# Layer 1, third wavelet level: five shifts on two quarters of the array, two partial sums added by the product above

## The chip, the cores and the metric

The kernel runs on one core of a Trainium2 chip. The metric is the device time of one execution in microseconds (us). Three runs of the kernel before took 5713.84, 5716.87 and 5730.83 us; the median is 5716.87. One more execution was taken with the profiler; it took 5714.57 us, and its profile spans 5712.6 us of that.

## The reference, cut to what matters

The program is four convolutional layers in sequence on 32 images of 96 channels, 56 by 56, each with a group norm in front and a residual sum behind. Layers 0, 2 and 3 are not touched. Layer 1 is a depthwise 5x5 convolution plus a three-level Haar wavelet transform, with a depthwise 5x5 convolution on the four bands of each level:

```
for i in range(3):
    co = haar2d(cur)                      # ll, lh, hl, hh at half the size
    cur = co[:, :, 0]                     # ll goes to the next level
    level_coeffs.append(dwconv(co, wconv_w[i]) * wscale[i])
next_ll = 0
for i in reversed(range(3)):
    co = level_coeffs[i]; co[:, :, 0] += next_ll
    next_ll = ihaar2d(co)                 # back up to twice the size
y = x + dwconv(x, base_w) * base_scale + base_b + next_ll
```

At the third level an input to the level is 14 rows by 14 columns for each image and channel.

## The kernel before

**How layer 1 is tiled.** Channels are taken in 48 pairs. In a pair, rows and column phases of an image lie on SBUF partitions and the 32 images on the free axis. A depthwise convolution down the rows is then a product with a banded (Toeplitz) matrix, one for each shift along the columns; TensorE adds the shifts in PSUM. All matrices are f32, and the profile shows every f32 product as two weight loads and two matmuls, which the text calls two passes. A product with f32r operands is one.

**The steps of a pair.** `lowest1` (L894) makes the input of level 2 out of `xh` and `xl`, two parts of the normalized image: `high` (ScalarE, L877) rounds `x` to `xh`, and `low` (VectorE, L881) makes `xl`, the rest. `lowest2` (L903) makes `x3`, the input of level 3, with the matrix `low2`: 112 rows by 56 columns, for both channels of the pair. `level3` (L910) forms five shifts with `T3`, a 56x56 block-diagonal matrix for each shift (channel 0 in rows and columns 0 to 27, channel 1 in 28 to 55), and ScalarE copies the sum to `c3` (L913). `level2` (L920), for each channel, forms three shifts and then adds the third level by one more product, `up2` times `c3` (L921), with 56 rows by 128 columns. The eviction of its sum is by halves: ScalarE copies a half, rounded (L926), then VectorE takes the rest (L927). `level1` (L938 for the product up, L932 for the three shifts) ends in `y`, which VectorE forms (L951) and SyncE's queue stores.

**What sets the order.** TensorE, VectorE, ScalarE and SyncE keep the order of the program here (`manual_schedule`). The loop at the end of `layer1` works on three pairs at a time: `far` is normalized, `nxt` goes through levels 2 and 3, and `i` through level 1. On TensorE one turn is: `lowest1(nxt)`, `level1(i, 0, 0)`, `lowest2(nxt)`, `level1(i, 0, 1)`, `level3(nxt)`, `level1(i, 1, 0)`, `level2(nxt, 0)`, `level2(nxt, 1)`, `level1(i, 1, 1)`. The first step of the next turn, `lowest1`, needs the `xl` that `low(far, 1)` makes, which on VectorE stands behind the four L927 of `level2`. On ScalarE `level3`'s copy is followed by the copies of `matrices1(far, 1)` (seven instructions, L748 and L775), then `high(far, 1)`, then the L926 of `level2`.

**Loads.** SyncE's queue issues all transfers of the layer. `load(i + 3)` brings, for each channel, the images, factors, matrices and, in `third` (L841), 28 rows of `T3`. Three sets of `T3`, `T2` and `c2` are filled with zeros by GpSimd when the layer begins (L820).

**Tiles on the array.** Layer 2's depthwise convolution already runs on four quarters of the array, 64 rows by 64 columns each. Its `quarter` picks row half `r` and column half `c`; in `depthwise` it is called as `quarter(ps[x], k, t, r, r ^ x, j, ...)`, so that for `x = 0` the quarters (0, 0) and (1, 1) write partitions 0 to 63 and 64 to 127 of the same PSUM tile, in the same half `j`, which is one bank. In layer 0 `project` runs eight tiles of 64 rows by 32 columns in f32 (the rows `hc,wg` of L548).

Of the kernel before, what the change touches and what calls it, by code (L numbers as in the profile page):

```python
# [10 lines left out]
F32 = mybir.dt.float32  # L11
BF16 = mybir.dt.bfloat16
F32R = mybir.dt.float32r
# [7 lines left out]
B, C, H, W = 32, 96, 56, 56  # L21
# [9 lines left out]
HH = H // 2  # L31
PH = HH * NPH
# [596 lines left out]
NK = 3  # L629
LEN = 2 * (HH + HALO) - 1  # L630
MIDL = HH + HALO - 1
KW = 5
# [100 lines left out]
def load_halves(nc, X, y):  # L733


    nc.sync.dma_start(X[:PH].rearrange("p h b q -> p h (b q)"), y.rearrange("(h p) b q -> p h (b q)", h=2))
    rows = y.rearrange("(t p r) b q -> t p r (b q)", t=NP, p=NPH)
    for h, v in enumerate((rows[2, :, :HALO], rows[1, :, -HALO:])):
        nc.sync.dma_start(X[PH:, h].rearrange("p b q -> p (b q)"), v)
# [11 lines left out]
def shifts(n, ks):  # L751


    for d in sorted(range(-(ks // 2), ks // 2 + 1), key=abs):
        yield ks // 2 + d, slice(max(0, -d), n - max(0, d)), slice(max(0, d), n + min(0, d))
# [5 lines left out]
def load_matrices(nc, pool, t, c, raw=None):  # L761

    if raw is None:
        raw = pool.tile([128, 2, NK * PH], F32, tag="raw", name="raw")
    nc.sync.dma_start(raw[:, 0], t[c, :128])
    nc.sync.dma_start(raw[LOW:PH, 1], t[c, LOW:PH])
    nc.sync.dma_start(raw[PH:, 1], t[c, 128:])
    return raw
# [11 lines left out]
def load_norm(nc, pool, norm, c):  # L780
    nr = pool.tile([128, 2 * B + 1], F32, tag="nr", name="nr")
    nc.sync.dma_start(nr, norm[c : c + 1, :].to_broadcast([128, 2 * B + 1]))
    return nr
# [3 lines left out]
def layer1(ctx, tc, w, y0, left, made, norm, t1, t2, t3, y1, k2, behind):  # L787
# [4 lines left out]
    nc = tc.nc  # L792
# [3 lines left out]
    pool = ctx.enter_context(tc.tile_pool(name="l1", bufs=2, reuse_waits="tile"))  # L796
    pfine = ctx.enter_context(tc.tile_pool(name="l1pf", bufs=4, space=PSUM, reuse_waits="tile"))
    psum = ctx.enter_context(tc.tile_pool(name="l1p", bufs=4, space=PSUM, reuse_waits="tile"))
    N2, N3 = W4 // 2, W4 // 2

    def constant(name, shape):
        t = cp.tile(shape, F32, tag=name, name=name)
        nc.sync.dma_start(t, w[name])
        return t

    def rounded(name, shape):

        t = cp.tile(shape, F32R, tag=f"{name}r", name=f"{name}r")
        nc.scalar.copy(t, constant(name, shape))
        return t  # L810
# [3 lines left out]
    for i in reversed(range(NF)):  # L814
        sets[i] = {
            name: cp.tile(shape, dtype, tag=f"{name}{i}", name=f"{name}{i}") for name, shape, dtype in (
                ("T3", [2 * HH, 2, HH * KW], F32), ("T2", [PH, 2, NK, 128], F32), ("c2", [128, 2, 2, N2, B], F32R))}
    for d in sets:
        for t in d.values():
            nc.gpsimd.memset(t.bitcast(F32) if t.dtype == F32R else t, 0.0)  # L820
# [1 line left out]
    def load(i):  # L822

        st = {"i": i, **sets[i % NF], "X": [], "T": [None] * 2, "nr": [], "raw": [], "raw2": [], "pf": {}}

        def images(c):
            X = io.tile([128, 2, B, W4], F32, tag="X", name="X", bufs=8)
            load_halves(nc, X, y0[c // GR][c % GR])
            st["X"].append(X)

        def factors(c):
            st["nr"].append(load_norm(nc, norms, norm, c))

        def matrices(c):
            st["raw"].append(load_matrices(nc, pool, t1, c))
            raw = pool.tile([PH, NK * PH], F32, tag="raw2", name="raw2", bufs=4)
            nc.sync.dma_start(raw, t2[c])
            st["raw2"].append(raw)

        def third(c):  # L840
            nc.sync.dma_start(st["T3"][c % 2 * HH : (c % 2 + 1) * HH, c % 2], t3[c])  # L841

        if i == 0:
            for c in range(2):
                matrices(c)
            left.issue(NP)
            for c in range(2):
                images(c)
            made.store(norm)
            for c in range(2):  # L850
                third(c)
            return st
        for c in (2 * i, 2 * i + 1):
            images(c)
            factors(c)
            matrices(c)
            third(c)
        left.issue(1)
        return st
# [38 lines left out]

    def lowest2(st):

        ps = psum.tile([2 * HH, N3, B], F32, tag="w", name="pa2")
        for j in range(2):
            nc.tensor.matmul(ps, low2[:, j, :], st["x2"][:, j], start=(j == 0), stop=(j == 1))  # L903
        st["x3"] = pool.tile([2 * HH, N3, B], F32, tag="x3", name="x3", bufs=2)
        nc.scalar.copy(st["x3"], ps)

    def level3(st):
        ps = psum.tile([2 * HH, N3, B], F32, tag="w", name="pc3")
        for n, (k, to, of) in enumerate(shifts(N3, KW)):
            nc.tensor.matmul(ps[:, to], st["T3"].rearrange("x c y -> x (c y)")[:, k::KW], st["x3"][:, of],  # L910
                             start=(n == 0), stop=(n == KW - 1))
        st["c3"] = pool.tile([2 * HH, N3, B], F32, tag="c3", name="c3", bufs=2)
        nc.scalar.copy(st["c3"], ps)  # L913

    def level2(st, j):

# [46 lines left out]
    def begin(st):  # L963
        for j in range(2):
            matrices1(st, j)
        for j in range(2):
            matrices2(st, j)
        both = cp.tile([128, 2, 2 * B + 1], F32, tag="nr0", name="nr0")
        made.spread(both, pick, psum.tile([128, 2, 2 * B + 1], F32, tag="w", name="pr0"))
        st["nr"] = [both[:, j, :] for j in range(2)]  # L970
        for j in range(2):
            for h in range(2):
                normal(st, j, h)
                st["pf"][j, h] = pfine.tile([128, W4, B], F32, tag="f", name="pc1")
                fine(st, j, h, True)
            high(st, j)
        for j in range(2):
            low(st, j)
# [3 lines left out]
    def do(step, i, *args):  # L982
        if i in sts:
            step(sts[i], *args)

    with tc.manual_schedule(engines=MANUAL_SP):
        low1 = rounded("low1", [128, 2, 2, 128])
        up1 = rounded("up1", [128, 2, 2, 128])
        low2 = constant("low2", [PH, 2, 2 * HH])
        up2 = constant("up2", [2 * HH, 2, 128])  # L990
        pick = constant("pick", [C, 2, 128])
        for i in range(-3, PAIRS):
            nxt, far = i + 1, i + 2
            if i + 3 < PAIRS:
                sts[i + 3] = load(i + 3)
            if far == 0:
                begin(sts[0])
                continue
            do(lowest1, nxt)
            do(normal, far, 0, 0)  # L1000
            do(matrices1, far, 0)
            do(normal, far, 0, 1)
            do(level1, i, 0, 0)
            do(lowest2, nxt)
            do(high, far, 0)
            do(low, far, 0)
            do(matrices2, far, 0)
            do(normal, far, 1, 0)
            do(level1, i, 0, 1)
            do(level3, nxt)  # L1010
            do(matrices1, far, 1)
            do(normal, far, 1, 1)
            do(high, far, 1)
            do(level1, i, 1, 0)
            do(level2, nxt, 0)
            do(level2, nxt, 1)
            do(matrices2, far, 1)
            do(low, far, 1)
            do(level1, i, 1, 1)
            sts.pop(i, None)  # L1020
            behind(i)
# [548 lines left out]
def lowest_bands():  # L1570

    low1 = np.zeros((PH + HALO * NPH, 2, 2, 128), np.float32)
    low2 = np.zeros((PH, 2, 2 * HH), np.float32)
    up1 = np.zeros((128, 2, 2, 128), np.float32)
    up2 = np.zeros((2 * HH, 2, 128), np.float32)

    def at(r, p):
        return PH // 2 * (r // 14) + 14 * p + r % 14  # L1580

    for r in range(HH):
        for p in range(NPH):
            for h in range(2):
                for n in range(2):
                    low1[at(r, p), h, n, at(HH // 2 * h + r // 2, 2 * n + p // 2)] = 0.5
            for c in range(2):
                low2[at(r, p), c, HH * c + 2 * (r // 2) + p // 2] = 0.5
    n = PH // 2
    for i in range(2):  # L1590
        for h in range(2):
            up1[64 * i : 64 * i + n, h, :, :PH] = low1[:PH, h, :, n * h : n * h + n].transpose(2, 1, 0)
        up2[:, :, 64 * i : 64 * i + n] = low2[n * i : n * i + n].transpose(2, 1, 0)
    return {"low1": low1, "low2": low2, "up1": up1, "up2": up2}


def layouts(a):
# [34 lines left out]
    def phase_taps(v):  # L1632
# [49 lines left out]
        "group": group.astype(np.float32),  # L1682
        "pick": np.repeat(np.eye(C, 2, dtype=np.float32)[:, :, None], 128, axis=2),
        **lowest_bands(),
        "grid": np.broadcast_to(grid, (C,) + grid.shape),
    }
# [23 lines left out]
```

## Time and profile before

| what | value |
|---|---|
| median of three runs | 5716.87 us |
| profiled execution | 5714.57 us, span 5712.6 us |
| layer 1 in the span | about 2640 to 3570 us |
| one turn of layer 1 (L894 to L894, 2997.66 to 3015.68) | 18.02 us |
| busy: TensorE, VectorE, ScalarE | 96%, 82%, 73% of the span |
| L903: 4 passes for each pair, 192 in all | 112x56 weights, 112x224 moving |
| L910: 10 passes for each pair, 480 in all | 56x56 weights; 224, 192 and 160 moving columns |
| L921: 4 passes for each pair, 192 in all | 56x128 weights, 56x224 moving |
| ScalarE copies from PSUM | 339 ns for 224 elements a partition (L905, L913), 532 ns for 448 (L897) |

A row of the costliest groups reads: line, engine, operation, output and inputs, the rows and columns of the weights (56*56), the shape and count; then the busy time in us, the mean of one in ns, and the idle time before it with what ended it. In a timeline a row is a start in us, a duration in us, and a group of instructions that follow each other; PE is a matmul, PEld a weight load. A matmul's end is modelled, so that the distance of starts says more than durations.

### The profile page before, as it was taken

Reading aid. Unit: us, or ns where it says so; the run is one execution under the profiler, and the core shown is the slowest. Engines: PE = TensorE matmul, PEld = TensorE weight load, DVE = VectorE, ACT = ScalarE, POOL = GpSimd, SP = SyncE. Lnnn points to the kernel's source line nnn. Section 1 sums busy time; section 2 is a strip of 40 time slices with the busy share of each in tenths; the row PEclk is TensorE's granted clock in tenths of the full one; section 3 lists DMA queues with packets and bytes.
Section 4 is the critical chain, followed back from the end, with each engine's and each line's share of the span. In section 5 each row is a group of like instructions: output and inputs, shape, how many; then the busy total and the mean of one; then the engine's idle time right before and its main releaser. Section 6 shows DMA issues by size and latency. Waiting matters only on the chain.

```text
span 5712.6 us, 137352 instructions
## 1 busy us (share of the span) xinstructions
PE 5494.4 (96%) x59704; PEld 3068.1 (54%) x59704; DVE 4692.3 (82%) x5413; ACT 4174.0 (73%) x6024; POOL 240.6 (4%) x158
## 2 busy tenths in 40 slices
PE   5999999999999999997999999899999999998999
PEld 2333333343343333333566665777788777776444
DVE  6999999999999999997776665777777777775777
ACT  5888888888888888884556654777777777676455
POOL 5000000000000000000000000000000000000000
PEclk9999999999999999998999999999999999999999
DMA  3123333332222332214577666479588796763888
GB/s 99 16 56 61 60 59 58 57 58 44 53 53 59 62 56 55 51 22 60 145 152 150 149 147 123 21 53 51 40 55 46 49 53 40 51 47 38 236 249 247
DMA packets 1285740, 454.45 MB, mean 80 GB/s; under 512 B 1102977, under 2 KB 1281081, under 8 KB 1283217
## 3 DMA queue, kind: packets, MB, share of 16 engines
q1 hardware_dynamic: 1285137, 445.68, 50.1%
q8 instruction: 468, 7.67, 0.6%
q14 instruction: 135, 1.11, 0.1%
HBM read 283.77 MB, written 214.08 MB: 87 GB/s over the span
## 4 chain that ended last, share of the span: by engine, by line
PE 81%; DMA 6%; ACT 4%; DVE 4%; issue 2%; SPq 1%; POOL 1%; ACTq 0%; DVEq 0%; POOLq 0%
PE psd L493 17%; PE psd L1291 13%; PE psj L548 10%; PE ps L426 7%; PE pc L932 7%; PE ps L1272 6%; PE pse L449 6%; PE psj L1334 3%; DMA X<-y 3%; PE pc L920 2%; ACT hi L1242 2%; PE pa L894 2%; PE pc L1466 2%; PE pc L910 1%; DMA raw<-tdiff 1%
## 5 line engine op out<-in xcount | busy, mean ns | idle before, releaser
L467 DVE SCALAR_TENSOR_TENSOR h<-hpad,l_wdw,h 128x3136 f32<-128x3136 f32 x512 | 1782.2, 3481 | 9.1
L493 PE MATMUL psd<-plane,filt 128*32 128x392 f32 (+5 forms) x16384 | 1083.6, 485 | 0.0
L1291 PE MATMUL psd<-apad,diag 64*64 64x392 bf16 x20736 | 916.2, 330 | 67.7 <-issue 63.8
L1291 PEld LDWEIGHTS <-diag 64*64 64x64 bf16 x20736 | 687.5, 106 | 291.7 <-issue 117.0
L493 PEld LDWEIGHTS psd<-plane,filt 128*32 128x32 f32 (+1 forms) x16384 | 390.7, 108 | 674.0 <-issue 621.6
L1262 ACT ACTIVATE u<-ps,o,s 128x784 int16<-128x784 f32 x576 | 536.4, 1002 | 163.9 <-PE ps L1272 145.0
L1262 ACT ACTIVATE a<-psd,o,s 128x784 int16<-128x784 f32 x448 | 423.6, 998 | 279.4 <-PE psd L1291 279.4
L748 ACT COPY T<-raw 128x112 f32<-128x112 f32 (+2 forms) x1386 | 445.6, 385 | 221.9 <-DMA raw<-tdiff 164.1
L426 PE MATMUL ps<-xn,l_wboth 96*128 96x392 f32 (+1 forms) x1536 | 465.2, 505 | 23.8 <-ACT xn L408 22.9
L467 DVE SCALAR_TENSOR_TENSOR hc<-hhalf,l_wdw,hc 128x1568 f32<-128x1568 f32 x256 | 473.7, 1850 | 16.1 <-ACT hc L460 9.5
L1272 PE MATMUL ps<-hi,l_w1q 96*128 96x392 f32 x1280 | 463.2, 362 | 6.8 <-DVE u L1260 3.7
L932 PE MATMUL pc<-x,T 128*112 128x416 f32 (+1 forms) x1152 | 447.3, 525 | 5.9 <-DVE x L870 5.9
L1272 PE MATMUL ps<-lo,l_w1q 96*128 96x392 f32 x1280 | 438.3, 342 | 2.9 <-DVE lo L1250 2.9
L1466 PE MATMUL pc<-x,T 128*112 128x416 f32 (+1 forms) x1152 | 419.4, 525 | 15.0 <-DVE x L1459 10.5
L449 PE MATMUL pse<-xn,l_wboth 96*32 96x392 f32 x4096 | 391.9, 501 | 3.6 <-ACT hab L470 3.6
L426 PEld LDWEIGHTS ps<-xn,l_wboth 96*128 96x128 f32 (+1 forms) x1536 | 219.5, 173 | 248.2 <-issue 53.6
L1466 PEld LDWEIGHTS pc<-x,T 128*112 128x112 f32 x1152 | 203.5, 178 | 230.4 <-issue 185.0
L470 ACT ACTIVATE hab<-psd,o,s 128x784 f32<-128x784 f32 x256 | 283.7, 1113 | 58.5 <-PE psd L493 56.1
L436 ACT ACTIVATE hpad<-ps,o,s 128x784 f32<-128x784 f32 x256 | 278.4, 1104 | 49.2 <-PE ps L426 47.8
L548 PE MATMUL psj<-h,wg 128*32 128x392 f32 x3072 | 307.1, 514 | 0.2 <-DVE wg L535 0.2
L548 PE MATMUL psj<-hab,wg 128*32 128x392 f32 x3072 | 304.8, 509 | 0.0
L453 ACT ACTIVATE plane<-pse,o,s 128x784 f32<-128x784 f32 x256 | 255.9, 1000 | 25.0 <-PE pse L449 20.3
(266 smaller groups left out, 7643.5 us busy)
## 6 DMA issues: line engine op xcount, KB each, us to landing
X<-y SPq DMA_DIRECT2D x192, 392.0 KB
y<-xt SPq DMA_DIRECT2D x108, 392.0 KB
y<-y SPq DMA_DIRECT2D x96, 392.0 KB
out_dram<-y SPq DMA_DIRECT2D x96, 392.0 KB
twav<-zwav SPq DMA_DIRECT2D x768, 36.8 KB
y<-kept SPq DMA_DIRECT2D x72, 392.0 KB
xt<-y SPq DMA_DIRECT2D x59, 392.0 KB
xt<-in_x_dram SPq DMA_DIRECT2D x8, 2352.0 KB
```

The costliest lines, as they stand in the source:

```text
L426: nc.tensor.matmul(ps[p, j, :NT], wexp[:, k * 128 : k * 128 + 128][:, m], im["xn"][:, j, rows, :].rearrange("c h w -> c (h w)"), start=Tru ...
L449: nc.tensor.matmul(ps[f * GC : (f + 1) * GC, half, :NT].rearrange("p (r w) -> p r w", w=W2), wexp[:, c : c + GC], im["xn"][:, f % 2, r0 : ...
L467: nc.vector.scalar_tensor_tensor(h2, taken(im, k, t), wdw[:, k, t : t + 1], h2, ALU.mult, ALU.add)
L470: nc.scalar.activation(view, ps, AF.Silu, bias=bi[1][:, c : c + 1], scale=sc[1][:, c : c + 1], accum_out=accum)
L493: nc.tensor.matmul(ps[at * GC : (at + 1) * GC, r, :NT].rearrange("p (r w) -> p r w", w=W2)[:, r0 - half * n : r1 - half * n, q0:q1], filt[ ...
L548: nc.tensor.matmul(ps[s * GC : (s + 1) * GC, t, :NT].rearrange("c (m r q) -> c r q m", m=2, q=W4), wg[p, k, c * GC : (c + 1) * GC], phases ...
L748: nc.scalar.copy(to.rearrange("x t (p s) -> x t p s", p=NPH), v[:, k])
L932: nc.tensor.matmul(ps[:PH, to], st["T"][j][:, h, k, :], st["x"][:, j, h, of], start=first and n == 0, stop=not first and n == NK - 1)
L1262: nc.scalar.activation(out, ps, AF.Identity, bias=o[:, c : c + 1], scale=s[:, c : c + 1])
L1272: nc.tensor.matmul(ps[:, j, :NT], w1[:, k * 128 : k * 128 + 128], im[part][:, r0 : r0 + RT, :].rearrange("c h w -> c (h w)"), start=(part ...
L1291: nc.tensor.matmul(ps[q, j, :NT].rearrange("p (r w) -> p r w", w=W), diag[p, k, t, :], v, start=(t == 0), stop=(t == 8))
L1466: nc.tensor.matmul(ps[:, :, to], st["T"][:, h, k, :], st["x"][:, h, :, of], start=(n == 0), stop=(n == NK - 1))
```

## The change

`low2` and `up2` get twice the columns and rows: each is padded from 56 to 64 and repeated, so `lowest2` writes `x3` twice, on partitions 0 to 63 and 64 to 127, and `up2` adds the two halves of `c3`. `T3` holds the block-diagonal matrix twice in the same way. The shifts `k` = 2, 3, 4 run on the quarter of rows and columns 0 to 63, `k` = 0, 1 on that of 64 to 127, into the two halves of one PSUM tile. The upper half's first column is not written by either of its two shifts, so the copy to `c3` leaves it out and `c3` becomes a tile of the set, filled with zeros once. `third` issues two transfers for each channel where it issued one.

```diff
-                ("T3", [2 * HH, 2, HH * KW], F32), ("T2", ...), ("c2", ...))}
+                ("T3", [128, 64 * KW], F32), ("T2", ...), ("c2", ...),
+                ("c3", [128, N3, B], F32))}
...
         def third(c):
-            nc.sync.dma_start(st["T3"][c % 2 * HH : (c % 2 + 1) * HH, c % 2], t3[c])
+            at, n = c % 2 * HH, HH * KW
+            for tile in range(2):
+                nc.sync.dma_start(st["T3"][64 * tile + at : 64 * tile + at + HH, at * KW : at * KW + n], t3[c])
...
     def lowest2(st):
-        ps = psum.tile([2 * HH, N3, B], F32, tag="w", name="pa2")
+        ps = psum.tile([128, N3, B], F32, tag="w", name="pa2")
...
     def level3(st):
-        ps = psum.tile([2 * HH, N3, B], F32, tag="w", name="pc3")
+        ps = psum.tile([128, N3, B], F32, tag="w", name="pc3")
         for n, (k, to, of) in enumerate(shifts(N3, KW)):
-            nc.tensor.matmul(ps[:, to], st["T3"].rearrange("x c y -> x (c y)")[:, k::KW], st["x3"][:, of],
-                             start=(n == 0), stop=(n == KW - 1))
-        st["c3"] = pool.tile([2 * HH, N3, B], F32, tag="c3", name="c3", bufs=2)
-        nc.scalar.copy(st["c3"], ps)
+            tile = slice(0, 64) if k >= KW // 2 else slice(64, 128)
+            nc.tensor.matmul(ps[tile, to], st["T3"][tile, k::KW], st["x3"][tile, of], start=(n < 2), stop=(n > 2))
+        nc.scalar.copy(st["c3"][:, 1:], ps[:, 1:])
+        nc.scalar.copy(st["c3"][:64, 0], ps[:64, 0])
...
-        low2 = constant("low2", [PH, 2, 2 * HH])
-        up2 = constant("up2", [2 * HH, 2, 128])
+        low2 = constant("low2", [PH, 2, 128])
+        up2 = constant("up2", [128, 2, 128])
...
+    def twice(v, axis):
+        v = np.pad(v, [(0, 8 * (a == axis)) for a in range(v.ndim)])
+        return np.concatenate([v, v], axis=axis)
+
+    return {"low1": low1, "low2": twice(low2, 2), "up1": up1, "up2": twice(up2, 0)}
```

In the compiled order, TensorE's and VectorE's instructions keep their number and places; ScalarE gets one more copy a pair, SyncE one more transfer a channel, GpSimd three more fills. Some transfers that layer 3 needs later (`xt<-tdiff`) stand at other places of SyncE's queue, and one small factor of layer 2 (L1094, L1095) stands behind GpSimd's reductions instead of before them.

More of the change, by code (lines that the diff above doesn't have):

```diff
@@ L816, in layer1 @@
             name: cp.tile(shape, dtype, tag=f"{name}{i}", name=f"{name}{i}") for name, shape, dtype in (
-                ("T3", [2 * HH, 2, HH * KW], F32), ("T2", [PH, 2, NK, 128], F32), ("c2", [128, 2, 2, N2, B], F32R))}
+                ("T3", [128, 64 * KW], F32), ("T2", [PH, 2, NK, 128], F32), ("c2", [128, 2, 2, N2, B], F32R),
+                ("c3", [128, N3, B], F32))}
     for d in sets:
@@ L899, in lowest2 @@
     def lowest2(st):
-        ps = psum.tile([2 * HH, N3, B], F32, tag="w", name="pa2")
+        ps = psum.tile([128, N3, B], F32, tag="w", name="pa2")
         for j in range(2):
             nc.tensor.matmul(ps, low2[:, j, :], st["x2"][:, j], start=(j == 0), stop=(j == 1))
-        st["x3"] = pool.tile([2 * HH, N3, B], F32, tag="x3", name="x3", bufs=2)
+        st["x3"] = pool.tile([128, N3, B], F32, tag="x3", name="x3", bufs=2)
         nc.scalar.copy(st["x3"], ps)
     def level3(st):
-        ps = psum.tile([2 * HH, N3, B], F32, tag="w", name="pc3")
+        ps = psum.tile([128, N3, B], F32, tag="w", name="pc3")
         for n, (k, to, of) in enumerate(shifts(N3, KW)):
-            nc.tensor.matmul(ps[:, to], st["T3"].rearrange("x c y -> x (c y)")[:, k::KW], st["x3"][:, of],
-                             start=(n == 0), stop=(n == KW - 1))
-        st["c3"] = pool.tile([2 * HH, N3, B], F32, tag="c3", name="c3", bufs=2)
-        nc.scalar.copy(st["c3"], ps)
+            tile = slice(0, 64) if k >= KW // 2 else slice(64, 128)
+            nc.tensor.matmul(ps[tile, to], st["T3"][tile, k::KW], st["x3"][tile, of], start=(n < 2), stop=(n > 2))
+        nc.scalar.copy(st["c3"][:, 1:], ps[:, 1:])
+        nc.scalar.copy(st["c3"][:64, 0], ps[:64, 0])
     def level2(st, j):
@@ L1593, in lowest_bands @@
         up2[:, :, 64 * i : 64 * i + n] = low2[n * i : n * i + n].transpose(2, 1, 0)
-    return {"low1": low1, "low2": low2, "up1": up1, "up2": up2}
+    def twice(v, axis):
+        v = np.pad(v, [(0, 8 * (a == axis)) for a in range(v.ndim)])
+        return np.concatenate([v, v], axis=axis)
+    return {"low1": low1, "low2": twice(low2, 2), "up1": up1, "up2": twice(up2, 0)}
 def layouts(a):
```

## The prediction

> **What bounds the kernel now.** I read the 40 slices first (TensorE at nine tenths in nearly all, layer 1 in slices 19 to 25), then the busy time by stretches, the chain of waits, and the timeline of one turn of layer 1.
>
> ```profile
> PE   5999999999999999997999999899999999998999
> ...
> 3000.00:3100.00 100.00, 99.97 (x388) 60.57 (x387) 68.31 (x100) 61.22 (x166) 0.00 (x0) 1.00 0.78 153
> ```
>
> The last line is a stretch of layer 1: 100 us, of which matmuls are busy 99.97, weight loads 60.57, VectorE 68.31, ScalarE 61.22; the granted clock is 1.00. The chain of waits in 2640 to 3600 is nearly all TensorE (L932 40%, L920 11%, L894 9%, L910 8%). So what TensorE saves in a turn is saved in the layer, until another engine is late. A busy matmul is not yet a useful one, so the turn has to be read closely:
>
> ```profile
> 3003.99 0.18 PEld L932 LDWEIGHTS pc<-x,T 128*112 128x112 f32 x1 [0.17 <-issue]
> 3004.34 0.18 PEld L932 LDWEIGHTS pc<-x,T 128*112 128x112 f32 x1 [0.17 <-issue]
> 3005.12 1.56 PEld L910 LDWEIGHTS pc<-x,T 56*56 56x56 f32 x10 [0.61 <-ACT T L748]
> 3006.88 0.30 PEld L938 LDWEIGHTS pc<-c,up1r 128*128 128x128 f32 x2 [0.19 <-issue]
> ```
>
> These are the weight loads alone, ahead of, in and behind level3. The level-2 part of the same turn, all engines, in order of time:
>
> ```profile
> 3009.35 1.19 PE L920 MATMUL pc<-x,T 112*128 112x224 f32 x6
> ...
> 3010.47 0.64 PE L921 MATMUL pc<-c,up 56*128 56x224 f32 x2
> ...
> 3011.04 1.30 PE L920 MATMUL pc<-x,T 112*128 112x224 f32 x6
> ...
> 3011.15 0.34 ACT L926 CAST c<-pc 56x224 fp32r<-56x224 f32 x1 [0.53 <-PE pc L921]
> ...
> 3012.27 0.64 PE L921 MATMUL pc<-c,up 56*128 56x224 f32 x2
> 3012.84 0.30 PEld L938 LDWEIGHTS pc<-c,up1r 128*128 128x128 f32 x2 [0.28 <-DVE c L927]
> ...
> 3014.54 1.09 DVE L881 TENSOR_TENSOR xl<-x,xh 128x896 fp32r<-128x896 f32 x1
> 3015.68 0.19 PEld L894 LDWEIGHTS pa<-xl,low1r 128*128 128x128 f32 x1 [0.53 <-DVE xl L881]
> ```
>
> **A column's price.** Two weight loads of L932 with 416 columns each are 0.35 us apart, so a pass costs 0.84 ns a column.
>
> **A change of shape costs 0.20 us.** L920 follows L932, both with over 64 rows and columns: 6 passes, 2x(224+192+192) = 1216 columns, 1.02 us. It starts at 3009.35 and L921's load at 3010.47: 1.12, so 0.10 us is lost ahead of L921. L921 (56 rows) has 448 columns, 0.38 us, and takes 0.57 to the next load: 0.19 lost. The second L920 takes 1.23 for the same 1.02: 0.21 lost. Each change between a 56-row or 56-column product and a full one thus costs 0.10 us until the array has run empty and 0.10 us until the first weights are in. The load of the next weights otherwise lies under the running pass.
>
> **The change part by part.**
>
> **lowest2** gets 128 weight columns instead of 56 and so the full shape. Now its four passes (896 columns, 0.75 us) take 0.90 from 3001.67 to L938's load, with another 0.09 before and 0.11 after: 0.35 us over the columns. A 128-column load lasts 190 ns (L920) against a 188 ns pass, so I leave 0.02. Saved: **0.33 us**.
>
> **level2's product up** gets 128 rows. Four changes of shape a turn (in and out of two L921) go: 4 x 0.20 = **0.80 us**.
>
> **level3** keeps its two changes of shape. Its columns are 2x(224+192+192+160+160) = 1856, 1.56 us. Afterwards the first quarter has k = 2, 3, 4: 2x(224+192+160) = 1152 columns, 0.97 us; the second 704, 0.59 us. If they run side by side, the first decides: **0.60 us** saved; if in turn, nothing. The order alternates (k = 2, 1, 3, 0, 4), and even a strict order, in which each pass waits for the one before it in its quarter, ends at the 0.97. For f32 the nearest row is layer 0's `hc,wg`:
>
> ```profile
> 2653.66 0.92 PE L548 MATMUL psj<-hc,wg 64*32 64x392 f32 x16
> ...
> L1291 PE MATMUL psd<-apad,diag 64*64 64x392 bf16 x20736 | 916.2, 330 | 67.7 <-issue 63.8
> ```
>
> Sixteen f32 passes of 392 columns are 16 x 0.33 = 5.3 us in turn and took 0.92: eight tiles ran together. But there the two row halves write different banks. The Trainium skill, page "TensorEngine Tiling (Array Packing)", section "Restrictions and Gotchas", speaks against this change: different row tiles cannot use the same PSUM bank at the same time. The change does just that. Yet layer 2's quarters do too: its quarters (0,0) and (1,1) write two halves of one bank, and 20736 bf16 products of 392 columns (0.165 us each: that far apart stand L1334's, of the same length, on the full array) took 916.2 us, 44 ns each, 3.7 at a time. With turns in a bank it could not be over two. By the rule level3 saves 0, by the row 0.60; I take the row.
>
> **ScalarE** copies c3 in two pieces. From 339 ns for 224 elements and 532 for 448: 0.86 ns each and 146 ns fixed, so 192 elements cost 311 and 32 cost 174: 0.15 us more. Behind them stand the seven copies of matrices1, then high, then L926. Now they take 3.64 us from 3006.99, and L926 starts at 4.16. Afterwards 3.8 of work lies in 3.96 (L921 comes one change earlier): hidden, with 0.15 to spare; uncovered it costs 0.15 x 48 = 7 us.
>
> **What is late next.** L894 already waits for xl (0.53 us in the last line above). The chain is: L921 of channel 0, four steps ACT, DVE, ACT, DVE, the same for channel 1, then L881. It ran from 3011.15 to 3015.68, 4.53 us. Channel 1's L921 comes 0.40 sooner after channel 0's (the two changes between them). Its first L926 then starts at 1.41 and its L927 at 1.78, free of channel 0's last L927, which ends at 1.56 (3012.31 plus 0.40): the chain takes 4.13 to 4.14. So of the three changes of shape inside this stretch, only two shorten it; the third, 0.20, becomes longer waiting at L894.
>
> **Sum of a turn**: 0.33 + 0.80 + 0.60 - 0.20 = 1.53, say 1.52 us, so 18.02 becomes 16.50. Over 48 turns 73 us. VectorE has some 12.3 us and ScalarE 11 us of work in a turn, which fits.
>
> **Loads.** SyncE issues two more T3 transfers a turn at 0.36 to 0.42 us, 0.8 us. In 2800 to 3440 (35.5 turns) it waited 205 us, 5.8 a turn; 18.0 - 5.8 + 0.8 = 13.0 of 16.5, so still covered. Behind third stand the stores of y and the next loads. Late data cost L894 one wait of 3.2 us near 2816, and TensorE 1.2 us near 3485, where transfers for layer 2 fill the queue; a faster layer meets them with less lead, so I add 3 us (bounds 0 and 10). Uncovered, the 0.8 us would be 40 us. The queue is also moved past a few xt<-tdiff of 21 KB, for layer 3: nothing. The three extra fills of GpSimd (c2's 896 elements take 0.84, so 0.2 each) come at 2668 to 2674; T2's, on which ScalarE waits, slips 0.05. The factor moved behind GpSimd's reductions is ready at about 2780, while layer 2 starts at 3570. The larger low2 and up2 are loaded under layer 0. All together nothing.
>
> **Total**: 5714.6 - 73 + 3 = **5645 us** against the profiled execution, which lies 2.3 below the median of the runs, inside their spread; I leave it so.
>
> **The rivals.**
>
> **A, the quarters take turns in the bank.** The skill's rule speaks for it, layer 2's row against it. level3 stays, 0.92 a turn remains: 44 us, 5670. Chance 0.11.
>
> **B, part of the saved changes of shape comes back as waits.** If the chain of L926 and L927 doesn't shorten (0.40: channel 0's four steps hold up channel 1's), 1.12 a turn remain, 54 us, 5664; if ScalarE is late too, by all of the first L921's 0.20, 0.92, 44 us, 5674. I say 5669. The 0.53 wait at L894 speaks for it; the 0.22 us of room between channel 0's last L927 and channel 1's first speaks against it. Chance 0.12.
>
> **C, slower: the load queue becomes the bound.** In the compiled order each issue waits for the transfer eight issues earlier; L841 has waited for an X load 12 times, 7.5 us in all. Two more issues a turn shift this window. An X load is 392 KB, 2.7 us at 147 GB/s. If each new issue waited for one whole, 2 x (0.42 + 2.7) = 6.2 us would go on top of SyncE's 12.2, a turn of 18.4: 48 x 0.4 = 19 us more, 5734. It decides from about 2.5 us of wait a new issue, where the old 5.8 of idle time a turn is used up (5.8 / 2 - 0.42). Against it: the mean wait now is 0.1 us. Chance 0.07.
>
> **D, nothing measurable**, by smaller waits of this kind that eat the gain: 5712, chance 0.06.
>
> **How the numbers follow.** My own case has 0.64. Its range: if the wait at L894 vanished, the turn could fall to 16.1, 92 us less 3 of late loads, 5626; if ScalarE slips (7), loads cost 10 and the f32 quarters overlap only to two thirds (0.2 x 48 = 10), 5669. Likeliest 5630 to 5662. For 8 in 10 the range takes in A and B: 5626 to 5683. This kernel's runs tell apart about 0.3%, 17 us. Faster by more than that: my case, A and B, 0.87; C slower, 0.07; D same, 0.06.
>
> **What would show it.** The distance of L894 to L894 falls to about 16.5 us. The loads after lowest2 and both L921 follow without the 0.20 us gaps: L920 to L920 1.40 us. level3 spans about 1.2 us from its first load to L938's load instead of 1.75, with passes of the two quarters overlapping; starts in strict turn would be rival A. The wait of L894 for xl grows to 0.7. SyncE still waits for L748 and L951. If layer 1's TensorE shows idle time and the turn stays at 18, I am wrong; if X or raw loads end VectorE's or ScalarE's waits, it is C.

## The result, and the profile after

Five runs of the changed kernel took 5647.33 to 5658.7 us, median **5648.74 us**; five of the kernel before 5702.1 to 5730.83, median 5713.84. The ratio is 0.9891, with a 95% interval of 0.9872 to 0.9910. The profiled execution took 5647.33 us and spans 5645.5. The forecast was 5645 us. The sum that led to it is right in its large terms and far too low in one small one, as follows.

The page shows TensorE and its granted clock in 40 slices of the span:

```profile
PE   5999999999999999998899999999999999999999
...
PEclk9999999999999999998999999999999999999999
```

Slice 19, in which layer 1 begins, stood at seven tenths before, with the clock at eight as here. New is the eight of slice 20, the first of layer 1 (nine before). Busy time in the same stretch of layer 1 for both kernels (length, TensorE, weight loads, VectorE, ScalarE, GpSimd, granted clock, DMA share, GB/s), first the kernel before, then the changed one:

```profile
2800.00:3400.00 600.00, 596.62 (x2312) 363.67 (x2312) 419.14 (x665) 356.48 (x958) 0.00 (x0) 1.00 0.67 148
```

```profile
2800.00:3400.00 600.00, 578.14 (x2440) 391.29 (x2441) 440.44 (x695) 380.44 (x1056) 0.00 (x0) 0.98 0.72 158
```

In the same 600 us there are 128 more matmuls and 98 more ScalarE instructions, but TensorE now stands still for 21.9 us instead of 3.4. (Some 35 of the 98 are the second copy to `c3`, one a turn.) The timeline of one turn (start, duration, engine, line) shows where the gain is:

```profile
2956.07 1.24 PE L914 MATMUL pc<-x,T 64*64 64x224 f32 x10
...
2957.24 0.48 PE L941 MATMUL pc<-c,up1r 128*128 128x224 f32 x2
2957.35 0.32 ACT L915 COPY c<-pc 128x192 f32<-128x192 f32 x1 [1.36 <-PE pc L914]
...
2957.57 0.18 ACT L916 COPY c<-pc 64x32 f32<-64x32 f32 x1
...
2959.71 1.19 PE L923 MATMUL pc<-x,T 112*128 112x224 f32 x6
...
2960.74 0.54 PE L924 MATMUL pc<-c,up 128*128 128x224 f32 x2
...
2961.12 1.19 PE L923 MATMUL pc<-x,T 112*128 112x224 f32 x6
...
2961.32 0.34 ACT L929 CAST c<-pc 56x224 fp32r<-56x224 f32 x1 [0.26 <-PE pc L924]
...
2965.47 0.47 PE L897 MATMUL pa<-xl,low1r 128*128 128x448 f32 x1 [0.20 <-DVE xl L884]
```

`level3` (now L914) begins at 2956.07 and the next product at 2957.24: 1.17 us, where it took 1.76 (5.12 to 6.88 in the prediction's rows). The first passes of its two quarters start 7 ns apart in the trace, and both write one PSUM bank. The two L923 are 1.41 us apart, where the two L920 were 1.69 apart. From L929 to `lowest1`'s xl (L897) it is 4.15 us; the weight load of that pass waits 0.73 us for xl (0.53 before, 0.7 forecast). A regular turn, from `lowest1` to `lowest1`, takes **16.54 us** instead of 18.03.

But some turns are longer. From the first `lowest1` of layer 1 to the last one (47 distances) it took 852.7 us before and 808.5 now: 44 us less, and not 47 x 1.49 = 70. I call **excess** what the turns from the sixth on have above the regular one, added up: 6.2 us before, 31.8 now.

### The profile page after: what moved, and what is told of

It is laid out like the page before. It is cut to its first block, busy times and chain, and to the rows that moved or that the text cites. A ratio compares the mean times of both kernels' runs of the same rounds, so it can differ in the third digit from the quotient of the medians.

```text
span 5645.5 us, 137543 instructions
## 1 busy us (share of the span) xinstructions
PE 5420.9 (96%) x59704; PEld 3086.1 (55%) x59704; DVE 4691.7 (83%) x5413; ACT 4179.3 (74%) x6072; POOL 240.3 (4%) x161
## 4 chain that ended last, share of the span: by engine, by line
PE 82%; ACT 5%; DVE 5%; DMA 4%; issue 2%; SPq 1%; POOL 1%; ACTq 0%; DVEq 0%; POOLq 0%
PE psd L493 18%; PE psd L1294 13%; PE psj L548 11%; PE ps L426 8%; PE ps L1275 7%; PE pse L449 6%; PE pc L935 5%; PE pc L1469 4%; PE psj L1337 4%; DMA X<-y 2%; ACT hi L1245 2%; PE pc L923 1%; PE pa L897 1%; ACT u L1265 1%; DVE xl L884 1%
## 5 line engine op out<-in xcount | busy, mean ns | idle before, releaser
L1294 PEld LDWEIGHTS <-diag 64*64 64x64 bf16 x20736 | 700.9, 106 | 262.8 <-issue 97.0
L748 ACT COPY T<-raw 128x112 f32<-128x112 f32 (+2 forms) x1386 | 445.9, 385 | 230.0 <-DMA raw<-tdiff 170.3
L935 PE MATMUL pc<-x,T 128*112 128x416 f32 (+1 forms) x1152 | 451.6, 529 | 6.1 <-DVE x L873 6.1
L1469 PEld LDWEIGHTS pc<-x,T 128*112 128x112 f32 x1152 | 203.2, 177 | 227.2 <-issue 188.7
L935 PEld LDWEIGHTS pc<-x,T 128*112 128x112 f32 x1152 | 193.6, 180 | 154.9 <-issue 154.9
```

Source lines behind the costliest of these rows:

```text
L748: nc.scalar.copy(to.rearrange("x t (p s) -> x t p s", p=NPH), v[:, k])
L935: nc.tensor.matmul(ps[:PH, to], st["T"][j][:, h, k, :], st["x"][:, j, h, of], start=first and n == 0, stop=not first and n == NK - 1)
L1294: nc.tensor.matmul(ps[q, j, :NT].rearrange("p (r w) -> p r w", w=W), diag[p, k, t, :], v, start=(t == 0), stop=(t == 8))
L1469: nc.tensor.matmul(ps[:, :, to], st["T"][:, h, k, :], st["x"][:, h, :, of], start=(n == 0), stop=(n == NK - 1))
```

## The experiments

Each profiled execution gives the turn, the excess and the length of layer 1 (first `lowest1` to the last of its f32 products). The last column is the distance from the first to the last depthwise product of layer 2, in which no experiment changes an instruction's work.

| kernel | median us | ratio to before, interval | turn | excess | layer 1 | layer 2 |
|---|---|---|---|---|---|---|
| before | 5713.84 | 1 | 18.03 | 6.2 | 880 | 1650 |
| changed | 5648.74 | 0.9891 [0.9872, 0.9910] | 16.54 | 31.8 | 834 | 1634 |
| e1_shape | 5678.73 | 0.9920 [0.9905, 0.9935] | 17.12 | 7.1 | 836 | 1656 |
| e2_one_quarter | 5682.32 | 0.9934 [0.9918, 0.9950] | 17.13 | 20.1 | 849 | 1651 |
| e3_low_first | 5613.73 | 0.9809 [0.9792, 0.9825] | 16.07 | 19.8 | 795 | 1639 |
| e4_spread | 5748.91 | 1.0052 [1.0037, 1.0067] | 18.09 (median) | 110 (over 16.54) | 915 | 1657 |
| e5_rows | 5640.07 | 0.9873 [0.9845, 0.9902] | 16.54 | 6.1 | 809 | 1653 |
| e6_merged | 5655.75 | 0.9903 [0.9877, 0.9928] | 16.54 | 15.9 | 819 | 1654 |
| e7_low_rows | 5604.82 | 0.9808 [0.9787, 0.9829] | 16.07 | 2.7 | 777 | 1643 |
| e8_after_again | 5666.53 (one run) | | 16.54 | 22.1 | 825 | 1659 |
| e9_before_low | 5691.61 | 0.9961 [0.9943, 0.9978] | 17.75 | 1.0 | 859 | 1633 |
| e10_before_again | 5727.7 (one run) | | 18.03 | 7.9 | 885 | 1656 |

The turn repeats to 0.01 us in all kernels that share the code of a turn; layer 2 scatters over 26 us between executions. So the turn and the excess tell the theories apart, and the medians alone do not below some 10 us.

### The shapes alone

`low2` and `up2` keep the full shape but are padded with zeros; the third level stays on one piece of the array, in one sum, with one transfer of `T3` a channel.

```diff
-    return {"low1": low1, "low2": twice(low2, 2), "up1": up1, "up2": twice(up2, 0)}
+    return {"low1": low1, "low2": np.pad(low2, [(0, 0), (0, 0), (0, 72)]), "up1": up1,
+            "up2": np.pad(up2, [(0, 72), (0, 0), (0, 0)])}
```

> The kernel before, with low2 and up2 padded by zeros to 128 columns and rows and nothing else: level3 keeps its five shifts of 56x56 one after the other, one transfer of T3 a channel. My theory (a change of shape costs 0.20 us, 0.20 of it given back at L894): the turn is 18.02 - 0.33 - 0.80 + 0.20 = 17.1 us, level3 still spans 1.75 us from its first load to L938's; over 48 turns 44 us, less some late loads, so about 5680 against the 5714 of the kernel before. Rival (all of the gain is the two quarters running together): the turn stays at 17.8 to 18.0 and the time at 5705 or more.

The turn is 17.12: the shapes alone bring 0.91 us. The prediction's own terms for them are 0.33 + 0.80 - 0.20 = 0.93. So the rival falls, and the time is as expected.

### All shifts on one quarter

The changed kernel, but the five shifts run on the quarter of rows and columns 0 to 63. The third level then comes from one sum, and the other half of `c3` stays zero.

```diff
-            tile = slice(0, 64) if k >= KW // 2 else slice(64, 128)
-            nc.tensor.matmul(ps[tile, to], st["T3"][tile, k::KW], st["x3"][tile, of], start=(n < 2), stop=(n > 2))
+            tile = slice(0, 64)
+            nc.tensor.matmul(ps[tile, to], st["T3"][tile, k::KW], st["x3"][tile, of], start=(n == 0), stop=(n == KW - 1))
```

> The changed kernel with all five shifts on the first quarter of the array, in one sum; the second half of c3 stays zero. All else is as in the changed kernel: shapes, copies of the same length on ScalarE, two transfers of T3. My theory (the quarters run side by side): the turn is 16.54 + 0.60 = 17.1 us and level3 spans 1.75 us again; 29 us slower than the changed kernel if loads were never late, less of it as far as the slower turn gives the loads their lead back, so 5655 to 5678. Rival (quarters take turns in the bank, the gain is elsewhere): the turn stays at 16.5 and the time at 5649.

Its `level3` and the product behind it, in the timeline:

```profile
2957.41 1.84 PE L914 MATMUL pc<-x,T 64*64 64x224 f32 x10
2959.17 0.48 PE L941 MATMUL pc<-c,up1r 128*128 128x224 f32 x2
```

1.76 us from start to start, against 1.17 in two quarters; the turn is 17.13 against 16.54. Two quarters are worth **0.59 us** a turn (predicted 0.60). Rival A, turns in the bank, falls, and with it, for this case, the rule of the Trainium skill (page "TensorEngine Tiling (Array Packing)", section "Restrictions and Gotchas") that stood against the row: two row tiles that write different partitions of one bank ran together.

Beside e1 it tells a second thing. Both have the same turn, 17.12 and 17.13, but e1 brings `T3` in one transfer a channel and e2 in two. The excess is 7.1 and 20.1 us. So 13 us more of late turns stand beside the two more issues a pair, at an equal turn. That is one profile of each, and two profiles of the changed kernel differ by 10 us (31.8 and 22.1), so it is an indication, not a measurement. The expectation that a slower turn gives the loads their lead back did not come true: 5682.32 us lies above its 5655 to 5678.

### low ahead of level 2 on VectorE

```diff
+            do(low, far, 1)
             do(level2, nxt, 0)
...
-            do(low, far, 1)
```

> The changed kernel with low(far, 1) put ahead of level2 in the order, so that VectorE makes xl before the four L927 of level 2 (L930 there) and not behind them. My theory (the chain through ScalarE and VectorE, not TensorE, sets the end of the turn): the wait of L894 (L897) for xl goes and the turn falls from 16.54 to 16.0 to 16.1 us. By itself that is 48 x 0.5 = 24 us; but the loads have still less lead, so that half of it or more is lost in late loads: 5625 to 5645. Rival (ScalarE or VectorE has no room for a shorter turn): the turn stays at 16.5.

The waits of 2690 to 3480 (engine, line, waited for: us, times, longest), first the changed kernel, then this one:

```profile
PE pa L897 <- DVE xl L884: 26.7, 45, 3.3
```

```profile
PE pa L897 <- DVE xl L884: 4.5, 6, 1.0
```

The wait stood in nearly every turn; six are left. The turn falls from 16.54 to 16.07, 0.47 us. The time, 5613.73, is below the expected 5625 to 5645: the excess, 19.8, did not grow with the shorter turn. The prediction named this chain (L926 and L927 twice each for each channel, then `low`) as what is late next, and gave 0.20 us of the gain back to it. To see what the same edit is worth without the change, it was put on the kernel before as well:

> The kernel before with only low(far, 1) ahead of level2, as in e3. There the chain ended some 0.3 us after TensorE was ready (matmul to matmul at L894; 0.53 for its weight load). My theory (the chain is nearly even with TensorE before, and the change makes it the later of the two): the turn falls by 0.3 to 0.35 us, from 18.02 to 17.7, 15 us in all, 5700; e3 took 0.47 a turn off the changed kernel. Rival (low first helps both alike): 17.55 and 23 us, 5691.

There it brings 18.03 to 17.75, **0.28 us**, as its theory had it. In all it brings 22 us by the ratio, where the theory had 15 and the rival 23: 13 come from the turns, and the rest from fewer long turns (the excess is 1.0) and a shorter start. The change made the edit worth 0.47: only after TensorE had become shorter was the chain late by that much.

### Where the late turns come from

Layer 2's input is copied in layer 1 already: every eight turns `Layer2.begin` issues two transfers of 16 channels, together 7168 packets of 112 bytes. SyncE's queue in the changed kernel, before the long turn from 2942.54 to 2964.57:

```profile
2910.74 0.62 SPq L1124 DMA_DIRECT2D kept<-y  x1
2911.41 4.92 SPq L1124 DMA_DIRECT2D xt<-y  x1
2916.37 6.72 SPq L736 DMA_DIRECT2D X<-y  x1
```

The issue of the second transfer lasts 4.92 us here (3.2 to 4.9 in the five cases) and that of the image load behind it 6.72, where an undisturbed `X<-y` takes 0.37. All loads behind are some 11 us later. VectorE then waits 3.96 us for a factor (L872, at 2930.85) and ScalarE 2.65 for a matrix (L748, at 2931.17); `high` ends at 2940.65. The stores of y stand in the same queue and are late too: L954, ahead of the L930 on VectorE, waits 2.07 us for one. `low`, behind the L930 of level 2, starts only at 2944.90. `lowest1` waits. Here are the rows of L954 and of `lowest1`, with two of L935 behind it:

```profile
2941.75 0.68 DVE L954 SCALAR_TENSOR_TENSOR y<-pc,nr,X 112x448 f32<-112x448 f32 x1 [2.07 <-DMA y<-y]
...
2946.05 0.74 PE L897 MATMUL pa<-xl,low1r 128*128 128x448 f32 x1 [2.82 <-DVE xl L884]
...
2949.23 3.79 PE L935 MATMUL pc<-x,T 128*112 128x448 f32 x6
...
2953.83 2.31 PE L935 MATMUL pc<-x,T 128*112 128x448 f32 x6
```

The two kernels' waits for loads in 2690 to 3480, before and changed:

```profile
DVE x L869 <- DMA nr<-norm: 10.8, 5, 3.7
...
ACT T L748 <- DMA raw<-twav: 4.5, 3, 2.5
```

```profile
DVE x L872 <- DMA nr<-norm: 21.8, 6, 5.7
...
ACT T L748 <- DMA raw<-twav: 16.6, 9, 4.5
```

And SyncE's two largest waits of its own, for ScalarE to free a buffer and for VectorE to make y; they are most of its slack. Before and changed:

```profile
SPq L765 <- ACT T L748: 111.6, 58, 6.0
SPq L958 <- DVE y L951: 97.5, 31, 4.0
```

```profile
SPq L765 <- ACT T L748: 64.3, 55, 5.5
SPq L961 <- DVE y L954: 61.2, 31, 3.0
```

Together they fell by 84 us, about 2.1 a turn; the shorter turn (1.5) and two more issues (0.8) make 2.3. So after a transfer for layer 2 the queue should need more turns to catch up. Three kernels test it, all on the changed one. The first two cut each of the two transfers into parts, one part a turn (two, if more than eight wait), by 4 channels or by 56 rows (the loop that issues them is left out):

```diff
-            for i, pair in enumerate(self.pairs):
-                self.nc.sync.dma_start(pair[g * GR : (g + 1) * GR], self.y1[g][:, :, 2 * i : 2 * i + 2, :])
+            self.parts += [(g, r, i) for i in range(2) for r in range(0, GR, 4)]               # e4
+            self.parts += [(g, r, i) for i in range(2) for r in range(0, H * NPH, PH // 2)]    # e5
```

> The changed kernel with the transfers for layer 2 (L1121, two of 16 channels each after every 8 turns) cut into eight of 4 channels, one a turn. In the changed kernel the turns that follow each pair of these transfers are 4 to 6 us too long, some 27 us in all. My theory (these bursts hold up the loads, which have too little lead for a turn of 16.5): the long turns at every eighth go, some 15 to 20 us less, 5630. Rival (SyncE's queue itself is too slow because of the two new T3 transfers a turn): the long turns stay or spread over all turns, 5645 to 5655.

> As e4_spread, but each transfer of 16 channels is cut by rows (56 of 224) and not by channels, one part a turn. In e4 a part of 4 channels had 896 packets where a whole one has 3584, and still held the queue about as long. My theory (a transfer over 4 channels keeps few of the DMA engines busy, so it lasts as long as one four times its size): parts with all 16 channels are four times shorter, the loads keep their lead, the long turns go: 5625 to 5640. Rival (every such transfer costs its 5 to 10 us in the queue, whatever its shape): as slow as e4, about 5749.

Cut by rows, the long turns are gone: behind the first ten turns, the 37 others add up to 0.1 us of excess, where the changed kernel has 25.7 and 16.0 in its two profiles. Layer 1 takes 809 us, and the time, 5640.07, is at the upper end of what was expected. Cut by channels, everything is late, against the expectation: the turn rises to a median of 18.09 us and the kernel is slower than before. The parts have 896 packets of 112 bytes in both. SyncE's queue in a turn with two parts, by channels and then by rows:

```profile
3004.57 5.42 SPq L1130 DMA_DIRECT2D xt<-y  x2
3010.04 5.74 SPq L736 DMA_DIRECT2D X<-y  x1
```

```profile
2992.02 1.64 SPq L1130 DMA_DIRECT2D xt<-y  x2
2993.70 0.93 SPq L736 DMA_DIRECT2D X<-y  x1
```

A part of 4 channels occupied the queues for 5 to 6.7 us, one of 16 channels and 56 rows for 1.1 to 2.4. (The Trainium skill, page "DMA: Bandwidth & Descriptors", section "Why a DMA increments its semaphore by 16 and not by 1", says that a transfer runs on the largest number of engines up to 16 that divides the slowest dimension of both sides. Here the channels are that dimension: 4 engines against 16. The trace agrees: at most 8 of these packets are in flight at once in e4, up to 27 in e5 and up to 32 in a whole transfer; the times are 2 to 6 apart.) So e4 is no test of whether spreading helps, but it shows the state that rival C describes, reached by another way: from 3000 us on SyncE waits for ScalarE's L748 only 2.6 us in all, no slack is left, and the turn is the queue's.

The third takes two issues a pair away instead: the two 16-row loads of a matrix become one.

```diff
-    nc.sync.dma_start(raw[LOW:PH, 1], t[c, LOW:PH])
-    nc.sync.dma_start(raw[PH:, 1], t[c, 128:])
+    n = NK * PH
+    src = t[c, LOW:PH]
+    nc.sync.dma_start(raw[LOW:, 1], bass.AP(src.tensor, src.offset, [[32 * n, 2], [n, 16], [1, n]]))
```

> The changed kernel with the two 16-row loads of raw in load_matrices made one transfer, so that SyncE issues as many transfers for a channel as in the kernel before; the bytes and packets are the same. Theory that the late loads come from the two new issues a turn (0.84 us of the queue): the 27 us of long turns fall to some 5 to 10, 5630. My theory (they come from the shorter turn against the transfers for layer 2; the issues are a small part): a few us, 5640 to 5649.

Its excess is 15.9 us, between e5's and the changed kernel's 22 and 32 in two executions. It has as many issues as the kernel before, and still some 9 us more excess; that points to the shorter turn as another part of the cause, but it is no more than the scatter of the excess. Against it stands e3: its turn is shorter still, 16.07, and its excess 19.8. The time of e6 (5655.75) is above both forecasts and not distinguishable from the changed kernel's. That the excess itself scatters, the two kernels once more show:

> The changed kernel once more, unedited, for its profile. Layer 1's turns (16.54, and 4 to 6 us more behind each group of transfers for layer 2) should be the same to 0.1 us. Layer 2, from its first to its last depthwise product, took 1649.6 us in the profile before and 1633.9 in the one after, without an edit there. Theory that this is scatter of an execution: it lies anywhere in 1630 to 1660 now. Rival (the change moves something in layer 2 for good): 1634 again, within 2 us.

> The kernel before once more, for its profile: layer 1's turns as in the first profile (18.02, and few long ones) to 0.1 us; layer 2 anywhere in 1630 to 1660 us, if it is scatter of an execution.

### Both edits together

e3 and e5 in one kernel:

> e3_low_first and e5_rows together. If cutting by rows keeps the loads ahead, the turn is 16.06 nearly everywhere and the time falls by the long turns that e3 still has (some 25 us): 5590 to 5605. If the cut transfers hold the queue as in e4, the time rises well over e3's 5614.

5604.82 us, ratio 0.9808 [0.9787, 0.9829] to the kernel before; the interval lies wholly under the changed kernel's. In the stretch shown at the start:

```profile
2800.00:3400.00 600.00, 600.00 (x2618) 415.98 (x2617) 468.64 (x736) 406.49 (x1125) 0.00 (x0) 1.00 0.68 168
```

TensorE has no idle time left in it, and every turn from the ninth on is 16.06 to 16.08 us. Layer 1 takes 777 us, 103 less than before. By the medians e3 (5613.73 on another chip) and e7 differ by 9 us, with layer 1 18 us apart.

## Why the prediction was right, and where not

**Shapes and the product up** (0.33 + 0.80): right; e1 shows 0.91 with the 0.20 taken off, by the prediction 0.93.

**level3 in two quarters** (0.60): right, 0.59 by e2. The choice of layer 2's row over the rule decided 29 us (0.60 x 48).

**The chain that is late next** (4.13 to 4.14, so 0.20 given back): right, 4.15, and its wait is the one that e3 took away. Rival B, by which the chain does not shorten, falls with it. (Rivals A and B each have a case with 0.92 us a turn left, at 5670 and 5674; A's leaves out the 3 us of late loads.)

**ScalarE's second copy** (0.15, hidden): right. The copies take 0.32 and 0.18; `high` ends before the first L929, which still waits 0.26 us for TensorE.

**The turn** (1.52): 1.49. Over 48 turns 71.5 us where the sum had 73.

**Late loads** (3 us, bounds 0 and 10): this is the term that was mis-sized. The excess grew from 6 to 8 us to 22 to 32, by **14 to 26 us**. The prediction had the right place ("transfers for layer 2 fill the queue; a faster layer meets them with less lead") but took the size from two waits of before. One of them, near 2816, was no late load. VectorE first made layer 2's weights; the last long row of that work in the kernel before is

```profile
2801.33 0.66 DVE L1081 TENSOR_SCALAR l_w3q<-xt 128x960 bf16<-128x960 f32 x1
```

and only at 2802.23 did it go on with the next pair. In e5, where VectorE and ScalarE wait for no load of the pairs (`nr`, `raw`), the same wait is there, 3.33 us. It stands in the seventh and eighth turn, which make 3 to 6 us of the excess in both kernels. Behind the tenth turn the excess is 1.3 and 4.7 us before, 25.7 and 16.0 changed: 11 to 24 us more. What failed is the step "still covered" for SyncE: it set the mean slack of a turn, 5.8 us, against 0.8 of new issues. In a regular turn that holds. But the slack is what pays back the 11 us that each pair of transfers for layer 2 costs every eight turns, and of it the shorter turn took 1.5 and the issues 0.8. That the transfers are the origin, e5 shows. How the growth divides between the shorter turn and the issues stays open: e1 beside e2 (13 us for the issues) and e6 (15.9) are single profiles. By the prediction's own sign, loads that end ScalarE's waits (`raw`: 3 times before, 9 changed), a part of rival C came true, but not by its mechanism: SyncE's L844 waited for X loads 13.6 us in all, 8.4 before, not the 2.5 us a new issue that C needs.

The price of a wait was missed as well. The long turn above is 22.03 us, 5.5 more than a regular one. The wait is only 2.82; the lower clock of the last section brings most of the rest.

**The total** came out near for a reason that is no merit of the sum. Layer 1 became shorter by 46 us in the first pair of profiles (880 to 834) and by 61 in the second (885 to 825), not 70. In the first pair layer 2 took 16 us less (1650 to 1634), the part behind layer 2 another 6, and with that the spans differ by 67. In the other ten profiles layer 2 takes 1633 to 1659 us, with and without the change, so I put these 16 us down to scatter; e8, with layer 2 at 1659, took 5666.53. That the change has a small lasting effect on layer 2 is not excluded.

## What to carry to other kernels

Read gains on the engine that bounds from the distances of weight loads, shape by shape: what a change of shape costs, and what two quarters save, followed to some hundredths of a microsecond. A queue's mean slack says nothing about a burst: before a stage is shortened, ask how many turns the largest rare transfer is paid back in, and cut it along a dimension that leaves every part wide. After the gain, move the next chain: the same line, `low` ahead of `level2`, was worth 0.28 us a turn before the change and 0.47 behind it.

## What the hardware did that I had not expected

TensorE's granted clock can fall to half around a wait of some 2 to 3 us. Around the long turn of the changed kernel (columns as above; the eighth figure is the clock):

```profile
2942.00:2946.00 4.00, 1.23 (x4) 0.37 (x2) 3.08 (x6) 1.88 (x6) 0.00 (x0) 0.92 0.68 191
2946.00:2949.00 3.00, 2.95 (x8) 2.65 (x9) 2.94 (x4) 0.00 (x0) 0.00 (x0) 0.50 0.73 160
2949.00:2953.00 4.00, 4.00 (x10) 2.03 (x9) 0.69 (x2) 2.81 (x8) 0.00 (x0) 0.60 0.50 121
2953.00:2957.00 4.00, 4.00 (x22) 2.64 (x21) 2.53 (x3) 2.15 (x5) 0.00 (x0) 1.00 0.88 287
```

Behind a wait of 2.82 us the clock stands at 0.50, then 0.60, for some 7 us. L897's passes come 0.37 us apart instead of 0.21 (seven distances, 1.1 us), and the six passes of L935 take 3.79 instead of 2.31 (1.5 us). With 2.6 us of wait beyond the regular 0.20 that is 5.2 of the 5.5. The kernel before has it too, behind its wait of 3.15 us near 2816:

```profile
2817.00:2820.00 3.00, 3.00 (x8) 1.91 (x7) 2.40 (x4) 2.05 (x6) 0.00 (x0) 0.50 0.74 191
```

The wait of every turn in the changed kernel, 0.20 us between its matmuls, leaves it at 1.00. The length of a wait alone does not decide. In e8, behind a wait of 1.80 us that ended at 2942.45, the clock is 0.50 in 2944 to 2946; in e10, the kernel before once more, the same wait of 3.15 us, ended at 2822.05, left it at 1.00, and so did one of 3.33 us in e1. What else decides, these runs do not show. So a rare wait of 3 us can cost nearly twice its length, as here.
